# Moving nine wide adjacency checks from VectorE in layer 0 to ScalarE in layers 2 and 3 of a four-layer graph network kernel

## The chip, the cores and the metric

The kernel runs on one core of a Trainium2 chip. The time is the device time of one launch in microseconds (us); several runs of a kernel give a median. A profiled execution has a time of its own and a span, which goes from its first to its last recorded instruction.

The engines are named as in the profile: PE (TensorE; PEld is its weight load), DVE (VectorE), ACT (ScalarE), POOL (GpSimd) and SP (SyncE, which here only issues transfers). Each engine works through its own queue in order: an instruction that waits holds up everything behind it on that engine.

## The reference, cut to what matters

A matrix `x` of 4096 rows and 64 columns goes through four layers of the form x = x + f(relu(layernorm(x)), adj). All four use the same 4096 x 4096 matrix `adj` of zeros and ones.

```python
# layer 0: attention masked by adj, rows scaled by their Lorentz norm
att = sigmoid((2 + 2 * (qm @ k.T)) / att_scale + att_bias)
support = (adj * att) @ h
x = x + support / denorm
# layer 1: entry j of a row weighs 0.5 ** (number of nonzero entries behind it), the last 100 count
x = x + (w @ (h @ weight) + bias)
# layer 2
Ax = adj @ h
x = x + (1.0 - 0.1 * h - 0.01 * sum(h * Ax, axis=1))
# layer 3
nb = adj @ h / maximum(deg, 1)
x = x + relu(concat([h, nb]) @ W.T)
```

## The kernel before

**Two models and a flag.** The kernel holds two versions of the network. The first keeps `adj` on the chip in an 8-bit form and relies on all entries being 0 or 1. The second takes any entries, and runs only if a flag says that some entry is neither. With these inputs it doesn't run. The flag needs each of the 256 tiles of `adj` (128 by 512 entries, f32) to be read once more in full precision and tested. Such a test is called a check. `fetch` (L426) takes the next tile from the deque `checks` and puts its load on SP's queue: one tile of 256 KB into a buffer `ck`, or two at once, 512 KB, into `ckw`. In the last stage the idle space of `s2a` gives two more wide buffers, so some wide checks appear in the profile as `s2a<-s2a`. `check` (L446) keeps loads ahead (three, and four in the last stage) and then has DVE test the oldest one with one instruction, which writes a count into a column of `odd`.

**Layer 0** goes over eight blocks `ib` of 512 rows (7 down to 0), each in 16 steps `g` of two 128-row tiles; the counter `k` numbers these 128 steps. A step has scores on PE (`ps`, L1059), a sigmoid on ACT (into `ps`, or into `att` for the first step in a group of four), a product with the mask on DVE, and, one group later, the sum on PE (`acc`, L1090). Three PSUM tiles hold the scores. `rows0` (L1020) turns the sums of a finished block into new rows, with small work on PE, ACT, DVE and POOL spread over the steps of the next block. POOL also issues the loads of the masks, one in each step (`load_masks`, L208). From step 33 on, the loop calls `check()` at five of every eight steps (L1234), narrow ones: 60 in all.

**Layer 1** counts and weighs entries (`cnt` L1500, `acc` L1535). `rows1` (L1314) makes the rows of a finished block and, in the same go, the inputs `s23` of layers 2 and 3. It is a chain over PE, ACT, POOL and DVE with three products of its own on PE (`pr`, `ph`, `pn`). It runs partly under the next stage.

**Layers 2 and 3** are summed together. `both_layers` (L1629) is one PE product (L1632), 1024 in all. `both_summed` (L1697) takes the row tiles in 16 pairs: the first six side by side over the first 28 of 32 steps, then each to its end, then the others one after another. The pairs use seven PSUM banks in turn. `need(2, t)` (L387) holds the writing of the program at step t until `rows1` of that block has been written out. After every eighth product `beat` (L1615) moves the pending jobs by one step, and at every second beat asks for one wide check on DVE. `last_rows` (L1657) finishes a pair: `high` on ACT, `agg`, `high`, `y` on DVE, `xm` on ACT, `y` on DVE, then the store.

**The flag.** `flagged` (L1287) is put among the jobs when the twelfth pair is written. When no check is left it sums `odd` into `bad` on DVE, four steps later PE adds it over the partitions (`pf`), DVE makes the flag, and all engines load it (L1725) while PE sums the last tile.

The program is written in a fixed order by hand (a manual schedule), so the order of the Python calls is the order on each queue. Almost all DVE and ACT instructions are recorded through one helper and carry its line, L73; they are told apart by their tiles.

Of the kernel before, what the change touches and what calls it, by code (L numbers as in the profile page):

```python
# [11 lines left out]
F32 = mybir.dt.float32  # L12
BF16 = mybir.dt.bfloat16
# [3 lines left out]
AF = mybir.ActivationFunctionType  # L17

GUESS, SHARE = 515594453.0, 0.0624625
ALU = mybir.AluOpType  # L20
AX = mybir.AxisListType
# [4 lines left out]
D = 64  # L26
P = 128
NT = N // P
IB = 512
NIB = N // IB  # L30
CI = IB // P
CG = 2
NG = NT // CG
# [45 lines left out]
def kernel(  # L79
# [12 lines left out]
    nc = tc.nc  # L92

    cpool = ctx.enter_context(tc.tile_pool(name="const", bufs=1))
# [19 lines left out]
    one = cpool.tile([P, 1], F32, name="one")  # L114
    nc.vector.memset(one, 1.0)
    eps = cpool.tile([P, 1], F32, name="eps")
    nc.vector.memset(eps, EPS)
    eps_up = cpool.tile([P, 1], F32, name="eps_up")
    nc.vector.memset(eps_up, EPS / UP / UP)

# [46 lines left out]
    def model(general):  # L167
# [4 lines left out]
        dve = Planned(nc.vector, clock, 0.07, 0.00105)  # L172
        act = Planned(nc.scalar, clock, 0.12, 0.00072)

        def pool(name, bufs, on=stack, **kw):
            return on.enter_context(tc.tile_pool(name=name + sfx, bufs=bufs, **kw))
# [25 lines left out]
        def get_mask(mp, ib):  # L202

            masks[ib] = mp.tile([P, NT, IB], FP8, name=f"mask{ib}{sfx}")
# [35 lines left out]
        def small(name, tag, on=epi, n=CI):  # L240
            return on.tile([P, n], F32, tag=name, name=f"{name}{tag}{sfx}")
# [128 lines left out]
        def push(job, lag):  # L370

            jobs.append([job, lag])
# [20 lines left out]
        def drain():  # L393
            while jobs:
                step()
# [9 lines left out]
        checks = deque(() if general else range(NIB * NT))  # L405
# [18 lines left out]
        fetched, made = deque(), [0]  # L424
# [21 lines left out]
        def check(tiles=1):  # L446


            for _ in range(1 if tiles == 1 else ahead[0] - len(fetched)):
                fetch(tiles)  # L450
            if fetched:
                k, at = fetched.popleft()
                dve.scalar_tensor_tensor(
                    at, at, 0.0, at, ALU.not_equal, ALU.not_equal, accum_out=odd[:, made[0] : made[0] + 1]
                )
                made[0] += 1
# [612 lines left out]
        def sigmoids(ps, to=None):  # L1069

            to = ps if to is None else to
            act.activation(to, ps, AF.Sigmoid, bias=att_c, scale=att_a)
            return to
# [119 lines left out]
        with tc.manual_schedule():  # L1193
            acc, late = first_rows_and_block()
            push(rows0(order0[0], evacuated(order0[0], acc, 0)), 10)
            pro_stack.close()
            mp1 = pool("mask_b", 1, side="right")
            for ib in order0[EARLY:]:
                get_mask(mp1, ib)
            spare.append(pool("pp1", 1, l0, space=PSUM))  # L1200
            if not general:
                push(count_constants(), 1)
            asking = iter(())

            def on():
                step()
                next(asking, None)

            sizes = [2] * 8 if general else [4] * 4
            first = [2] * 7 if general else [4, 4, 3, 3]
            sizes = first + (NIB - 2) * sizes + [0]
            k, done = NG + 2, NG
            LEAVING = {112 - 4 * ib: ib for ib in range(NIB)}
            for size in sizes:
                now = []
                for n, (ib, g) in enumerate(todo[k : k + size]):
                    edge[0] = n == size - 1
                    ps = scores(ib, g)  # L1220

                    if size > 2 and not now:
                        att = frm = sigmoids(ps, att_tile(ib, g))
                    else:
                        frm, att = sigmoids(ps), att_tile(ib, g)
                    masked(ib, g, frm, att)
                    now.append((ib, g, att))
                    load_masks(1)
                    k += 1
                    if k == 92 and not general:  # L1230
                        push(count_constants_2(), 1)
                    if not general and k in LEAVING:
                        taken(LEAVING[k])
                    if k > 2 * NG and k % 8 in (0, 2, 4, 5, 7):  # L1234
                        check()
                    on()
                for ib, g, att in late:
                    at = done % NG
                    if at == 0:
                        acc = pa0.tile([P, IB], F32, tag="pa", name=f"acc0_{ib}{sfx}")  # L1240
                        if ib > 0:
                            asking = queries(ib - 1)
                    gather(acc, fb, g, att, at)
                    if at == NG - 1:
                        push(rows0(ib, evacuated(ib, acc, 0)), 10)
                    done += 1
                late = now
            edge[0] = True
            if len(checks) % 2:
                check()  # L1250
            if general:
                drain()
# [12 lines left out]
        evac = pool("evac", 1)  # L1265
# [21 lines left out]
        def flagged(flag):  # L1287

            steps = 7 if general else 4
            while checks or fetched:  # L1290
                yield
            bad = small("bad", "")[:, 0:1]
            dve.tensor_reduce(bad, odd, AX.X, ALU.add)
            for _ in range(steps):
                yield
            pf = pm.tile([P, CI], F32, tag="pr", name="pf")
            nc.tensor.matmul(pf[0:1, 0:1], bad, one, start=True, stop=True)
            yield
            dve.tensor_scalar(flag, pf[0:1, 0:1], 1.0, None, ALU.min)
# [227 lines left out]
        with tc.manual_schedule():  # L1527
# [45 lines left out]
            late, k, moved, due = None, 0, False, 0.0  # L1573
# [38 lines left out]
        SKEW = 1  # L1612
        summed, beats = [0], [0]

        def beat():  # L1615
            step()
            beats[0] += 1
            if beats[0] % 2:
                check(2)

        flag, any_odd = None, []

        LEAD, SPLIT, PAIR = 6, 28, 2
        BANKS = (2, 5, 6, 0, 1, 3, 4)
# [32 lines left out]
        def last_rows(acc, tiles, tag, begun=None):  # L1657

            n, last = len(tiles), begun is not None
            h, xm = begun or rows_begun(tiles, tag)  # L1660
            high, agg = (
                ends.tile([P, n, 2, D], F32, tag=a, name=f"{a}_{tag}", bufs=2)
                for a in ("high", "agg")
            )
            y = ends.tile([P, n, D], F32, tag=f"y{last}", name=f"y_{tag}", bufs=2)
            inn = ends.tile([P, n], F32, tag="inn", name=f"inn_{tag}", bufs=2)
            act.activation(high, acc[:, 0:n, 0::2, :], AF.Copy, scale=STEP / UP)
            if not last:
                yield
            dve.scalar_tensor_tensor(  # L1670
                agg, acc[:, 0:n, 1::2, :], 1.0 / UP, high, ALU.mult, ALU.add
            )
            if not last:
                yield
            for j, t in enumerate(tiles):
                dve.scalar_tensor_tensor(
                    high[:, j, 0, :], agg[:, j, 0, :], -0.01 / UP, h[:, j, :],
                    ALU.mult, ALU.mult, accum_out=inn[:, j : j + 1],
                )
                dve.scalar_tensor_tensor(  # L1680
                    y[:, j, :], agg[:, j, 1, :], rdegs[:, t : t + 1], fa[:, t, :],
                    ALU.mult, ALU.add,
                )
            if not last:
                yield
            for j in range(n):
                act.activation(xm[:, j, :], xm[:, j, :], AF.Identity, bias=inn[:, j : j + 1])
            if not last:
                yield
            dve.scalar_tensor_tensor(y, y, 0.0, xm, ALU.max, ALU.add)  # L1690
            if not last:
                yield
            rows = slice(tiles[0], tiles[0] + n)
            (nc.scalar if last else nc.gpsimd).dma_start(out=out[:, rows, :], in_=y)
            yield
# [36 lines left out]
        if not general:  # L1732
            with tc.manual_schedule():
                for n in range(2):
                    free = q_sb[:, n * NT // 2 : (n + 1) * NT // 2, :]
                    more.append(free.rearrange("p (c a) d -> p c (a d)", c=CG))
                ahead[0], counting[0] = 4, False
                ends = pool("ends", 1, l2)
                both_summed()
            l2.close()  # L1740
            stack.close()
            return any_odd
# [169 lines left out]
```

## Time and profile before

| what | us |
|---|---|
| median of 3 runs (572.57 to 573.76) | 573.25 |
| the profiled execution | 572.18 |
| its span | 569.5 |
| PE busy | 552.0 (97%) |
| DVE busy | 467.5 (82%) |
| ACT busy | 358.8 (63%) |
| POOL busy | 272.2 (48%) |
| 60 narrow checks on DVE (`ck`) | 42.8, and 4.7 to read their counts |
| 76 wide checks on DVE (`ckw`) | 96.0, and 6.0 |
| 22 wide checks on DVE (`s2a`) | 27.6, and 1.7 |
| 1024 products of layers 2 and 3 (L1632) | 114.0 |

On the time line layer 0 reaches from about 58 to 296 us, layer 1 to about 444, layers 2 and 3 to 563, and the last rows and their stores to the end. PE's share of busy time is modelled and can hide short waits inside a group; waits between groups are shown in brackets on the time line.

### The profile page before, as it was taken

To read this page: it belongs to the slowest core of one execution; us is meant where nothing else is said; L and a number is where in the kernel's file an instruction comes from. 1 tells how busy PE (TensorE), PEld (TensorE's weight loads), DVE (VectorE), ACT (ScalarE), POOL (GpSimd) and SP (SyncE) were. 2 spreads that over 40 slices of the span, in tenths; PEclk is the share of its full clock that TensorE was granted. 3 is DMA by queue.
4 is the path that set the end of the run, shared out by engine and by line. 5 is a ranking of instruction groups with operands and counts; after the bars stand their busy time and mean duration, and the time that the engine had idled before them with its cause. 6 is when DMAs were issued, how large, how long until landed. Compare 5 with 4: busy or idle time off the path is not lost.

```text
span 569.5 us, 9915 instructions
## 1 busy us (share of the span) xinstructions
PE 552.0 (97%) x3368; PEld 280.8 (49%) x3368; DVE 467.5 (82%) x949; ACT 358.8 (63%) x663; POOL 272.2 (48%) x526
## 2 busy tenths in 40 slices
PE   8999999999999999999999999999999999999995
PEld 3563333333333333333334444445454788888884
DVE  4679657799999999898976877778969897799993
ACT  3677667766676776778741888988888432342231
POOL 7624402675757576754444510384634343334332
PEclk9999999999999999999999999999999999999998
DMA  8995952689999999994223465453544788859960
GB/s 145 133 106 47 100 50 20 57 131 154 150 169 150 166 126 173 152 158 121 74 89 113 151 209 168 132 170 112 155 145 132 241 266 304 274 190 323 343 251 21
DMA packets 45612, 87.86 MB, mean 154 GB/s; under 512 B 6272, under 2 KB 24576, under 8 KB 45552
## 3 DMA queue, kind: packets, MB, share of 16 engines
q1 hardware_dynamic: 26112, 69.14, 36.5%
q0 software_dynamic: 18912, 17.77, 33.0%
q8 instruction: 28, 0.46, 0.3%
q10 hardware_dynamic: 528, 0.23, 0.2%
q14 instruction: 32, 0.26, 0.2%
HBM read 135.60 MB, written 1.05 MB: 240 GB/s over the span
## 4 chain that ended last, share of the span: by engine, by line
PE 70%; DVE 13%; POOL 5%; ACT 5%; issue 3%; DMA 2%; DVEq 0%; ACTq 0%; POOLq 0%; SPq 0%
PE acc L1090 15%; PE acc L1632 15%; PE ps L1059 15%; PE acc L1535 8%; PE cnt L1500 8%; PE idle L1183 3%; DVE att L73 3%; DVE ckw L73 2%; PE many L1387 1%; DMA s2a<-adjt_dram 1%; DVE s2a L73 1%; ACT ps L73 1%; DVE rrq L73 1%; POOL mask L211 1%; PE pt L266 1%
## 5 line engine op out<-in xcount | busy, mean ns | idle before, releaser
L1059 PE MATMUL ps<-qt,kt 64*128 64x512 f32 x512 | 123.4, 610 | 3.4 <-DVE att L73 3.0
L1090 PE MATMUL acc<-att,fb 128*64 128x512 f32 x512 | 117.8, 599 | 0.6 <-DVE att L73 0.5
L1632 PE MATMUL acc<-s,mask 128*128 128x256 f16 x1024 | 114.0, 273 | 0.4 <-DVE s L73 0.4
L73 ACT ACTIVATE w<-cnt 128x512 int16<-128x512 f32 x187 | 98.6, 606 | 12.1 <-PE cnt L1500 11.0
L1632 PEld LDWEIGHTS <-mask 128*128 128x128 fp8e4 x1024 | 99.8, 98 | 13.0 <-issue 1.0
L73 DVE TENSOR_TENSOR att<-ps,mask 128x1024 f32<-128x1024 f32 x82 | 98.6, 1217 | 8.6 <-ACT ps L73 8.5
L73 DVE SCALAR_TENSOR_TENSOR ckw<-ckw 128x1024 f32<-128x1024 f32 x76 | 96.0, 1274 | 4.2 <-DMA ckw<-adjt_dram 4.2
L73 ACT ACTIVATE ps<-ps,att_c,att_a 128x1024 f32<-128x1024 f32 x82 | 93.8, 1175 | 1.3 <-PE ps L1059 0.8
L73 ACT ACTIVATE att<-ps,att_c,att_a 128x1024 f32<-128x1024 f32 x46 | 54.6, 1202 | 54.1 <-PE ps L1059 53.9
L1059 PEld LDWEIGHTS ps<-qt,kt 64*128 64x128 f32 x512 | 44.8, 186 | 79.0 <-issue 28.7
L211 POOL DMA_DIRECT2D mask<-adjt_dram x128 | 70.1, 560 | 19.1 <-DMA mask<-adjt_dram 17.4
L73 DVE TENSOR_TENSOR att<-att,mask 128x1024 f32<-128x1024 f32 x46 | 56.9, 1252 | 18.8 <-ACT att L73 18.5
L1500 PE MATMUL cnt<-mask,after 128*128 128x512 fp8e4 x256 | 67.4, 379 | 2.7 <-DVE two L73 0.8
L1090 PEld LDWEIGHTS acc<-att,fb 128*64 128x64 f32 x512 | 33.5, 136 | 73.0 <-issue 67.6
L1535 PE MATMUL acc<-w,s2a 128*128 128x512 bf16 x256 | 66.2, 379 | 1.2 <-ACT asb L73 1.2
L73 DVE TENSOR_SCALAR w<-cnt 128x512 int16<-128x512 f32 x69 | 46.9, 686 | 22.6 <-PE cnt L1500 22.2
L301 POOL TENSOR_TENSOR rs_a<-rs_y 128x4 f32<-128x4 f32 x48 | 19.1, 398 | 67.4 <-DVE rs_y L73 61.0
L73 DVE SCALAR_TENSOR_TENSOR ck<-ck 128x512 f32<-128x512 f32 x60 | 42.8, 713 | 0.0
L1535 PEld LDWEIGHTS <-s2a 128*128 128x128 f16 x256 | 24.6, 98 | 33.6 <-issue 5.6
L1500 PEld LDWEIGHTS <-after 128*128 128x128 bf16 x256 | 24.4, 99 | 31.0 <-issue 2.7
L73 ACT ACTIVATE xm<-xm,inn 128x64 f32<-128x64 f32 x32 | 10.4, 347 | 45.9 <-DVE high L73 44.2
L1183 PE MATMUL idle<-ones 128*128 128x512 bf16 x126 | 30.9, 401 | 1.6 <-DVE ones L73 1.6
(248 smaller groups left out, 611.9 us busy)
## 6 DMA issues: line engine op xcount, KB each, us to landing
ckw<-adjt_dram SPq DMA_DIRECT2D x76, 512.0 KB, 4.3
mask<-adjt_dram POOLq DMA_DIRECT2D x128, 128.0 KB, 8.7
ck<-adjt_dram SPq DMA_DIRECT2D x60, 256.0 KB, 5.9
s2a<-adjt_dram SPq DMA_DIRECT2D x22, 512.0 KB, 4.9
x_sb<-x_dram SPq DMA_DIRECT2D x4, 256.0 KB, 7.5
out_dram<-y POOLq DMA_DIRECT2D x15, 64.0 KB, 3.7
apart_m<-mask SPq DMA_DIRECT2D x16, 16.0 KB, 4.1
mask<-apart_m SPq DMA_DIRECT2D x16, 16.0 KB, 4.3
```

The source lines that it names most:

```text
L73: return op(out, *args, **kw)
L211: nc.gpsimd.dma_start(out=masks[ib][:, g * CG : (g + 1) * CG, :], in_=adjt[ib, g])
L266: nc.tensor.transpose(pt[:, c, :], part, ident)
L301: nc.gpsimd.tensor_tensor(a, y, y, ALU.mult)
L1059: nc.tensor.matmul(ps[:, c, :], kt[half, g, :], qts[ib][half, :], start=True, stop=True)
L1090: nc.tensor.matmul(acc[c * D : (c + 1) * D, :], lhs[:, t, :], rhs[:, c, :], start=(at == 0), stop=(at == NG - 1), skip_group_check=True,)
L1183: nc.tensor.matmul(v.idle[:, v.filling % CG, :], ones, ones.unsqueeze(1).to_broadcast([P, IB // P, P]), start=True, stop=True, skip_group_ ...
L1387: nc.tensor.matmul(pc[q * NT : (q + 1) * NT, :], lane[:, NT - 1 - t : 2 * NT - 1 - t], masks[quad * QUAD + q][:, t, :], start=(t == 0), st ...
L1500: nc.tensor.matmul(cnt, by, what, start=True, stop=True, skip_group_check=True)
L1535: nc.tensor.matmul(accs[ib], apart_s if t < 0 else both(s2a, t), w, start=(t == NT - 1), stop=False, skip_group_check=True,)
L1632: nc.tensor.matmul(acc[:, to, :, :].rearrange("p k d -> p (k d)"), masks[ib][:, t, c * P : (c + 1) * P], s23[:, t, :, :].rearrange("p k d ...
```

## The change

Eighteen of the 60 narrow checks of layer 0 are dropped: the loop checks at seven of every 16 steps, no more ten. The 18 tiles are instead taken from the end of the deque when layers 2 and 3 begin, as nine pairs. For each pair SP loads 512 KB into one buffer `cka`. Five beats later ACT starts four passes over it, each followed by a pause of a beat (the last by none): Relu(a - 1), Relu(-a), Sign(a) and Sign(1 - a), each with a sum over the entries into one column of `act_sums`. The values themselves go to `act_unused`, which shares its space with the buffer `asb` of layer 1. The load of the next pair is written one beat after the last pass, and waits for that pass, as there is one buffer. DVE's checks of layers 1 to 3 stay as they are, 98 wide ones.

The flag takes in the new sums: `flagged` also waits for `tested`, and `oddness` adds six small DVE instructions behind `bad`. To make room, `agg` has one buffer instead of two; it is written and read by DVE alone.

```diff
@@ -115,6 +115,8 @@
+    less = cpool.tile([P, 1], F32, name="less")
+    nc.vector.memset(less, -1.0)
@@ -1231,7 +1233,7 @@
-                    if k > 2 * NG and k % 8 in (0, 2, 4, 5, 7):
+                    if k > 2 * NG and k % NG in (0, 2, 5, 8, 10, 12, 13):
                         check()
@@ -1287,10 +1289,12 @@
-            while checks or fetched:
+            while checks or fetched or not (general or tested):
                 yield
             bad = small("bad", "")[:, 0:1]
             dve.tensor_reduce(bad, odd, AX.X, ALU.add)
+            if not general:
+                oddness(bad)
@@ -1612,13 +1616,54 @@
+        passes = iter(())
+
         def beat():
             step()
             beats[0] += 1
             if beats[0] % 2:
                 check(2)
+            next(passes, None)
 
         flag, any_odd = None, []
+        BY_ACT, FIRST_PASS = 9, 5
+        tested = []
+
+        def tested_by_act():
+            sums = ends.tile([P, 4, BY_ACT], F32, name="act_sums")
+            unused = evac.tile([P, CG * IB], BF16, tag="asb", name="act_unused", bufs=1)
+            for n in range(BY_ACT):
+                k = by_act.pop() - 1
+                by_act.pop()
+                at = ends.tile([P, CG * IB], F32, tag="cka", name=f"cka_{k}", bufs=1)
+                nc.sync.dma_start(out=at, in_=adjt[k // NT, k % NT // CG].rearrange("p c i -> p (c i)"))
+                for _ in range(FIRST_PASS):
+                    yield
+                for m, (func, bias, scale) in enumerate(
+                    ((AF.Relu, less, 1.0), (AF.Relu, 0.0, -1.0), (AF.Sign, 0.0, 1.0), (AF.Sign, one, -1.0))
+                ):
+                    nc.scalar.activation(
+                        unused, at, func, bias=bias, scale=scale, accum_out=sums[:, m, n : n + 1]
+                    )
+                    yield
+                    if m < 3:
+                        yield
+            tested.append(sums)
+
+        def oddness(bad):
+            out, signs = (small(f"act_{a}", "", ends, 1) for a in ("out", "signs"))
+            sums = tested[0]
+            dve.tensor_reduce(out, sums[:, 0:2, :], AX.XY, ALU.add)
+            dve.tensor_reduce(signs, sums[:, 2:4, :], AX.XY, ALU.add)
+            good = float(BY_ACT * CG * IB)
+            dve.tensor_scalar(out, out, 0.0, None, ALU.not_equal)
+            dve.tensor_scalar(signs, signs, good, None, ALU.not_equal)
+            dve.tensor_tensor(bad, bad, out, ALU.add)
+            dve.tensor_tensor(bad, bad, signs, ALU.add)
@@ -1659,8 +1704,8 @@
             high, agg = (
-                ends.tile([P, n, 2, D], F32, tag=a, name=f"{a}_{tag}", bufs=2)
-                for a in ("high", "agg")
+                ends.tile([P, n, 2, D], F32, tag=a, name=f"{a}_{tag}", bufs=bufs)
+                for a, bufs in (("high", 2), ("agg", 1))
             )
@@ -1736,6 +1781,8 @@
                 ends = pool("ends", 1, l2)
+                by_act = [checks.pop() for _ in range(CG * BY_ACT)][::-1]
+                passes = tested_by_act()
                 both_summed()
```

In the built program nothing else moves: PE's and POOL's instructions stand in the same order as before, DVE loses the 18 checks and gains the memset and the six instructions behind `bad`, ACT gains 36 passes between its others and no load of a function table, and SP loses 18 loads of 256 KB in layer 0 and gains nine of 512 KB behind layer 1.

## The prediction

> **What bounds the kernel now.** I read first the busy time by stage (stretch; its length; busy us of PE, PEld, DVE, ACT and POOL; granted clock; DMA share; GB/s).
>
> ```profile
> 183.00:214.00 31.00, 30.38 (x138) 10.56 (x136) 28.29 (x49) 21.08 (x24) 21.28 (x47) 1.00 1.01 153
> ...
> 445.00:480.00 35.00, 34.04 (x314) 29.53 (x312) 30.76 (x67) 10.81 (x58) 12.78 (x15) 1.00 0.85 276
> ...
> 520.00:540.00 20.00, 20.00 (x185) 17.93 (x184) 19.90 (x51) 4.61 (x15) 7.27 (x10) 1.00 0.98 343
> ```
>
> PE sets the pace: one block of layer 0 leaves it 0.6 us idle in 31, the last stage nothing. DVE is nearly full in both. ACT has room in the last stage (4.6 us busy of 20), which is where the passes go; but DMA is full there (0.98), and the passes need loads.
>
> Next, PE's waits in layer 0, on its time line:
>
> ```profile
> 178.62 1.99 PE L1059 MATMUL ps<-qt,kt 64*128 64x512 f32 x8 [0.77 <-DVE att L73]
> ...
> 209.56 1.99 PE L1059 MATMUL ps<-qt,kt 64*128 64x512 f32 x8 [0.62 <-DVE att L73]
> ...
> 264.49 1.99 PE L1059 MATMUL ps<-qt,kt 64*128 64x512 f32 x8 [0.68 <-DVE att L73]
> ```
>
> The name DVE misleads at the first two. The time line of all engines ahead of 209.56:
>
> ```profile
> 204.18 0.67 POOL L332 TENSOR_TENSOR xc<-x_sb,st 128x256 f32<-128x256 f32 x1
> ...
> 204.88 0.42 ACT L73 ACTIVATE sq<-xc 128x256 f32<-128x256 f32 x1 [1.88 <-POOL xc L332]
> ...
> 206.39 1.22 DVE L73 TENSOR_TENSOR att<-ps,mask 128x1024 f32<-128x1024 f32 x1 [0.89 <-ACT ps L73]
> ```
>
> POOL's `xc` is late, behind five mask issues (2.7 us from 201.48); ACT's `sq` waits for it, two sigmoids stand behind `sq`, and DVE itself waits 0.89 us before the product that PE needs. At 264.49 it is DVE: a check stands directly ahead of the product (262.54, 0.74 us).
>
> Third, the seam into layers 2 and 3, where the chain of waits runs through DVE and one load:
>
> ```profile
> 445.64 8.09 DMA s2a<-adjt_dram
> ```
>
> and on the time lines of ACT and PE:
>
> ```profile
> 450.47 0.42 ACT L73 ACTIVATE s<-fa 128x256 f32<-128x256 f32 x1 [4.61 <-POOL fa L332]
> 450.79 0.35 ACT L73 COPY ht<-ph 128x256 f32<-128x256 f32 x1
> ```
>
> ```profile
> 452.21 0.71 PE L1367 MATMUL pn<-wln_sb,ht 64*128 64x128 f32 x8
> ```
>
> PE needs `ht` 1.07 us after ACT has it. Last, the flag, on the time line of the end:
>
> ```profile
> 555.18 0.34 DVE L73 TENSOR_REDUCE bad<-odd 128x1 f32<-128x176 f32 x1
> ...
> 556.05 0.09 PEld L1297 LDWEIGHTS pf<-one,bad 128*1 128x1 f32 x2 [0.21 <-issue]
> ```
>
> `bad` is ready 0.5 us before PE takes it, and 64 products (7.1 us) and the tail (6.2 us) stand behind `pf`. DVE has had no pause since 510.
>
> **Layer 0: gain 1.5 us (0 to 5.5).** Eighteen checks of 0.713 and 0.079 us are 14.2 us of DVE. What PE can gain is far less. From the transposes of one block to the next take 30.36, 31.09, 30.94, 31.32 and 31.02 us, together 154.7; PE's own work in a block is 4 x 7.22 (a group of scores and one of sums) + 0.96 (transposes) = 29.84, five times 149.2. So 5.5 us is the ceiling. Dropped are, of each 16 steps, the checks behind steps 3, 6 and 14 counted from 0. Behind step 6, DVE then only waits longer at step 8 (0.66 us now, for ACT and so for PE). The chain that ends at 209.50 starts from that step, through two kept checks, `rs_y`, and POOL; a shorter DVE before and after moves nothing in it. I count the wait at 264.49, which has a dropped check right ahead (0.7), and some 0.2 us in each of four blocks where a group of scores takes 3.9 us and not 3.65: 1.5. At the ends of the layer nothing: PE is busy without a pause from 276 to 296. Dropping 18 loads from SP's queue there hides behind the same work, since no mask is waited for.
>
> **The passes as such: 45 us of ACT, hidden.** No row has this pass. The nearest, by form (busy us and mean ns):
>
> ```profile
> L73 ACT ACTIVATE ps<-ps,att_c,att_a 128x1024 f32<-128x1024 f32 x82 | 93.8, 1175 | 1.3 <-PE ps L1059 0.8
> ...
> L73 ACT COPY tq<-ps_q 128x1024 f32<-128x1024 f32 x4 | 4.0, 1012 | 1.3 <-PE ps_q L733 1.3
> ...
> L73 ACT ACTIVATION_READ_ACCUMULATOR s<-fa 128x1 f32 x16 | 3.0, 187 | 0.0
> ```
>
> Bounds are 1.01 and 1.18 + 0.19 = 1.37 us; I take 1.25, as reading the sum partly overlaps the next. 36 x 1.25 = 45 us go into about 76 idle us of ACT (111 less 35 busy). Three passes in a pair of 6.26 us take 3.75, rows 1.75: it fits. If it did not, `high` would be late, then `agg` on DVE, then `bad`.
>
> The Trainium skill ("ScalarE: Activation LUTs", What ACT_TABLE_LOAD costs) gives 186 ns + 0.833 a column, 93 more for a pointer operand, and 93 of overlap. By that an estimate is 0.95 to 1.04 us a pass, 36 us in all, and each stall below 0.2 us shorter. Its Rules for kernel authors also send relu to VectorE, which speaks against this move; what it costs in idle ACT time, the trace here says is nothing.
>
> **The first pass at the seam: loss 4.0 us (0.4 to 6.0).** The load of the first pair goes out right behind the `s2a` load above, at about 446.05. The first pass stands in ACT's queue between the two lines shown, so ACT reaches it at 450.9. It can start when the load is in: 451.0 by the median of such loads (4.9 us), 456.5 if it follows the `s2a` load of 453.73 as that one followed the one before (DVE got that at 450.97, 2.76 earlier). I take one load's 0.52 MB at 0.35 MB/us behind 453.73, so 455.2: the neighbour in the same queue is the nearer row. Pass 1.25 and `ht` 0.35 end at 456.8; PE, waiting with `pn` since 452.21, loses 4.6. Queued behind: on PE all products, on ACT `sq`, the copies, and, behind the second pass, `kept`, which DVE wants at 456.99 and gets near 460.5. So DVE's chain slides too (3.5), and PE's later waits in this stretch (0.53 and 0.43) repay only about 0.6: 4.0. PE has no idle time from 485 to 563 to win it back.
>
> **The end: loss 3.2 us (0.7 to 6.0).** Two things meet. DMA: about three of the nine loads fall into 515 to 535. There 338 GB/s are moved, 6.8 MB; with 1.6 more it is 8.3 MB, which at 0.35 to 0.368 MB/us (the best five us of the stage) takes 22.7 to 23.8 us. From 535 to 550 hardly any room is left. So DVE's last check comes 1.9 to 3.7 us late, taken 2.5. The six instructions behind `bad`: two sums of about 0.2, four small ones at 0.17 to 0.19 and their gaps, 1.2 us. Less the 0.5 us of slack: 3.2. The low end is the six alone; the high end adds 1.5 us of DVE waiting for `high` behind a pass. Behind `pf` nothing is hidden.
>
> The skill ("DMA: Bandwidth & Descriptors", Specifications) puts the limit of one core's reads at about 358 GB/s; the stage's best five us show 368, so it is no strict wall here. By it the checks would come about 3 us late.
>
> `less` hides under the first loads of x; the single `agg` is written and read in DVE's order and costs gaps of 0.04 us at most.
>
> Sum: 572.18 - 1.5 + 4.0 + 3.2 = 577.9. The profiled execution is 1.1 below the median, so the median becomes 578.9.
>
> **Rivals.** *The load is early.* If it lands by 451.3 (the median says so, its neighbour against), the seam costs 0.4: 573.25 - 1.5 + 0.4 + 3.2 = 575.4.
> *Layer 0 pays.* If DVE's backlog, and not POOL, carries PE's pauses from block to block, up to all 5.5 us of excess comes back. For: DVE is 28.3 busy of 31, and the first block with checks throughout ran 0.7 us quicker than the next ones, as if a backlog built up. Against: DVE's own waits of 0.66 and 0.89. Full price with both losses at their low ends: 573.25 - 5.5 + 0.4 + 0.7 = 568.9; with 4.0: 570.4. It decides once the gain passes the losses, so only together with a seam that costs little.
> *SP is held up.* The next `cka` load waits on SP for the last pass, with DVE's loads behind it. DVE's loads have some 0.4 us to spare (three checks of 1.57 us against 4.3 to land), so an ACT that runs 0.8 us behind in eight turns adds up to 8 x 0.4 = 3.2 more, and both ends high: 573.25 - 1.5 + 6.0 + 6.0 + 3.2 = 587.0.
>
> **How the numbers follow.** Forecast 0.56, early load 0.14, layer 0 pays 0.19, SP held up 0.11. Within 0.2% (1.1 us, about what can be told from no change) counts the early load with a short end, 0.06; faster 0.18; slower 0.76. For 8 in 10 I cut the far part of the third case and of the last: 570.8 to 585.0. The forecast's own range, with its three terms halfway to their bounds, is 575 to 582.
>
> **What would show it.** Right: one PE wait of 3 to 6 us at `pn` near 452 put down to ACT `ht`, with ACT idle before the first pass on DMA; waits of DVE for `ckw` or `s2a` loads past 515; PE waiting at `pf` for `bad`; blocks of layer 0 still near 31 us. Wrong: blocks near 30 us, or a first pass that starts at once.

## The result, and the profile after

The changed kernel takes 586.89 us (median of 6 runs, 585.09 to 589.92) against 572.88 for the kernel before in the same runs: 1.0245 times, with a 95% interval of 1.0225 to 1.0265. The forecast was 578.9 us with a range of 570.8 to 585.0: the sign and the places were right, the size was not. The profiled execution took 585.09 us, the shortest of the six, with a span of 583.3, which is 13.8 more than the span before.

First the stretches of the changed kernel, in the columns used above (the stretch, its length, busy us of PE, PEld, DVE, ACT and POOL, granted clock, DMA share, GB/s):

```profile
183.00:214.00 31.00, 30.61 (x138) 10.61 (x134) 27.32 (x43) 21.10 (x24) 20.98 (x48) 1.00 0.96 133
445.00:480.00 35.00, 30.43 (x270) 26.48 (x269) 25.80 (x57) 18.67 (x71) 11.47 (x15) 0.95 0.78 261
520.00:540.00 20.00, 20.00 (x186) 17.93 (x185) 17.71 (x47) 13.34 (x31) 4.38 (x9) 1.00 0.97 374
```

Layer 0 is little changed: DVE has 1 us less to do in 31, and PE is 0.4 us idle, not 0.6. From 445 to 480 PE has lost 3.6 us of work (30.43 busy, 34.04 before) and its granted clock is below 1. From 520 to 540 PE loses nothing, but DVE is 2.2 us less busy than before (17.71, 19.90): it waits, at a time when DMA moves 374 GB/s.

The seam into layers 2 and 3, on the time lines of ACT and then PE:

```profile
453.61 1.15 ACT L1647 ACTIVATE act_unused<-cka,less 128x1024 bf16<-128x1024 f32 x1 [4.70 <-DMA cka<-adjt_dram]
454.66 0.19 ACT L1647 ACTIVATION_READ_ACCUMULATOR act_unused<-cka,less 128x1 f32 x1
454.75 0.35 ACT L73 COPY ht<-ph 128x256 f32<-128x256 f32 x1
```

```profile
455.16 0.89 PE L1371 MATMUL pn<-wln_sb,ht 64*128 64x128 f32 x8 [4.57 <-ACT ht L73]
```

ACT stands 4.70 us before its first pass until the load is in, and PE waits 4.57 us for the `ht` behind that pass. The end, on PE's time line:

```profile
554.73 4.42 PE L1677 MATMUL acc<-s,mask 128*128 128x256 f16 x39
567.29 0.19 PE L1301 MATMUL pf<-one,bad 128*1 128x1 f32 x2 [8.14 <-DVE bad L73]
567.41 9.20 PE L1677 MATMUL acc<-s,mask 128*128 128x256 f16 x64
```

PE waits 8.14 us for `bad`, where it had none to wait for before, and the 64 products behind `pf` take 9.20 us instead of 7.16. So the span's 13.8 us are made up of these: layers 2 and 3 begin 1.70 earlier (442.38, 444.08 before), the last `pn` comes 3.04 later (484.10, 481.06), so the seam cost 4.74; then 8.14 at `pf`, 2.04 in the products behind it and 0.5 in the tail. The sum 3.04 + 8.14 + 2.04 + 0.5 is 13.7.

Why `bad` is late is read from DVE's waits between the start of layers 2 and 3 and `bad` (us in total, times, the longest). Before, then after:

```profile
DVE y L73 <- DMA out_dram<-y: 3.4, 4, 2.2
DVE rs L73 <- ACT rs L73: 1.9, 1, 1.9
DVE s L73 <- POOL s L286: 1.6, 1, 1.6
DVE agg L73 <- ACT high L73: 1.6, 1, 1.6
DVE s2a L73 <- DMA s2a<-adjt_dram: 0.9, 1, 0.9
DVE ckw L73 <- DMA ckw<-adjt_dram: 0.8, 1, 0.8
```

```profile
DVE y L73 <- DMA out_dram<-y: 5.7, 4, 2.0
DVE va L73 <- ACT rs L73: 4.3, 1, 4.3
DVE agg L73 <- ACT high L73: 3.8, 3, 2.0
DVE ckw L73 <- DMA ckw<-adjt_dram: 3.4, 4, 1.2
DVE rs L73 <- ACT rs L73: 1.9, 1, 1.9
DVE s2a L73 <- DMA s2a<-adjt_dram: 1.7, 1, 1.7
DVE s L73 <- POOL s L288: 0.7, 1, 0.7
DVE kept L73 <- ACT kept L73: 0.7, 1, 0.7
```

With the short ones, these come to 10.2 us before and 22.3 after. The way from the start of the stage to `bad` became 12.8 us longer (111.1 to 123.9), so nearly all of it is waiting: 5.0 for what stands on ACT behind the first load (`rs`, `kept`), 3.3 for DVE's own loads, 2.3 for stores of `y`, 2.3 for `high`, less 0.9 for `s`. DVE is the engine that has no room in this stage: its work and these waits fill nearly the whole way, so what it waits longer shows in `bad`. The 8.14 us of PE's wait follow from it: 12.8, and 0.7 for the six instructions behind `bad`, less the 4.74 that PE itself had lost at the seam and the 0.5 of slack before, come to 8.3.

And ACT's longest group of waits after the change, in the same stretch:

```profile
ACT act_unused L1647 <- DMA cka<-adjt_dram: 21.3, 7, 4.7
```

### The profile page after: what moved, and what is told of

It is laid out like the page before. It is cut to its first block, busy times and chain, and to the rows that moved or that the text cites. A ratio compares the mean times of both kernels' runs of the same rounds, so it can differ in the third digit from the quotient of the medians.

```text
span 583.3 us, 9920 instructions
## 1 busy us (share of the span) xinstructions
PE 553.7 (95%) x3368; PEld 283.3 (49%) x3368; DVE 457.7 (78%) x920; ACT 397.9 (68%) x735; POOL 265.0 (45%) x526
## 3 DMA queue, kind: packets, MB, share of 16 engines
HBM read 135.60 MB, written 1.05 MB: 234 GB/s over the span
## 4 chain that ended last, share of the span: by engine, by line
PE 58%; DVE 14%; ACT 9%; DMA 9%; POOL 5%; issue 4%; ACTq 0%; SPq 0%; DVEq 0%; POOLq 0%
PE acc L1092 15%; PE ps L1061 14%; PE acc L1539 8%; PE cnt L1504 8%; PE acc L1677 6%; DMA cka<-adjt_dram 5%; DVE att L73 4%; ACT act_unused L1647 3%; DVE ckw L73 3%; DMA out_dram<-y 2%; PE many L1391 1%; ACT ps L73 1%; DMA vec<-vecs_dram 1%; ACT w L73 1%; PE pr L1326 1%
## 5 line engine op out<-in xcount | busy, mean ns | idle before, releaser
L1677 PE MATMUL acc<-s,mask 128*128 128x256 f16 x1024 | 116.7, 277 | 0.0
L1677 PEld LDWEIGHTS <-mask 128*128 128x128 fp8e4 x1024 | 101.2, 99 | 13.8 <-issue 0.7
L73 DVE TENSOR_TENSOR att<-ps,mask 128x1024 f32<-128x1024 f32 x82 | 98.0, 1218 | 10.2 <-ACT ps L73 9.9
L303 POOL TENSOR_TENSOR rs_a<-rs_y 128x4 f32<-128x4 f32 x48 | 16.7, 347 | 67.5 <-DVE rs_y L73 61.0
L73 DVE SCALAR_TENSOR_TENSOR ck<-ck 128x512 f32<-128x512 f32 x42 | 30.8, 734 | 0.0
L73 DVE SCALAR_TENSOR_TENSOR s2a<-s2a 128x1024 f32<-128x1024 f32 x22 | 27.1, 1242 | 1.7 <-DMA s2a<-adjt_dram 1.7
```

Source lines behind the costliest of these rows:

```text
L73: return op(out, *args, **kw)
L303: nc.gpsimd.tensor_tensor(a, y, y, ALU.mult)
L1677: nc.tensor.matmul(acc[:, to, :, :].rearrange("p k d -> p (k d)"), masks[ib][:, t, c * P : (c + 1) * P], s23[:, t, :, :].rearrange("p k d ...
```

## The experiments

Three explanations of the late `bad` were open. *Loop*: with one buffer, each load is written only after the last pass, ACT then stands before it at the head of its queue (21.3 us in all), and what it owes DVE is late. *DMA*: the nine loads take room that DVE's loads and the stores need. *ACT's time*: the passes themselves are too long. Medians are set against the kernel before in the same set of runs. The last two columns are of the profiled execution alone: for kernels 2, 3, 4 and 10 that was the longest of its runs (1.9, 3.6, 1.8 and 2.5 us above the median), for the change and kernel 8 the shortest (1.8 and 1.3 below). Where kernels of different sets are compared, two differences are given: that of the medians, and that of the column "less before", as the kernel before itself came out between 572.88 and 573.76.

| kernel | median us | less before | ratio, 95% interval | PE waits at pf | 64 products behind |
|---|---|---|---|---|---|
| the change | 586.89 | +14.0 | 1.0225 to 1.0265 | 8.14 | 9.20 |
| 1 layer 0 alone | 572.18 | -1.0 | 0.9966 to 1.0010 | 0.68 | 7.16 |
| 2 loads alone | 578.79 | +5.6 | 1.0056 to 1.0105 | 5.47 | 9.90 |
| 3 passes alone | 572.84 | -0.3 | 0.9967 to 0.9996 | 3.12 | 8.83 |
| 4 two buffers | 588.30 | +15.1 | 1.0219 to 1.0274 | 10.78 | 9.82 |
| 5 four y | 583.68 | +9.9 | 1.0145 to 1.0203 | 5.76 | 9.06 |
| 6 first pass later | 584.18 | +10.4 | 1.0158 to 1.0219 | 9.87 | 8.53 |
| 7 seam, y and flag | 578.99 | +5.2 | 1.0075 to 1.0133 | 3.21 | 10.02 |
| 8 before, four y | 572.87 | -0.9 | 0.9978 to 1.0000 | 0 | 7.16 |
| 9 as 7, passes packed | 580.72 | +7.2 | 1.0110 to 1.0153 | 3.13 | 10.00 |
| 10 the change, wait filled | 584.67 | +11.2 | 1.0170 to 1.0204 | 2.69 | 7.16 |
| 11 six pairs | 573.45 | 0.0 | 0.9986 to 1.0011 | 0 | 7.16 |
| 12 as 7, wait filled | 576.76 | +3.9 | 1.0047 to 1.0088 | 1.52 | 7.16 |

**Kernels 1 to 3: the parts by themselves.** Layer 0 alone:

```diff
-            while checks or fetched or not (general or tested):
+            while checks or fetched:
...
-            if not general:
-                oddness(bad)
...
-                passes = tested_by_act()
```

> The changed kernel with the 18 checks dropped from layer 0 and nothing put in their place: no loads, no passes and no six instructions behind bad, so 18 tiles are not tested at all. All theories of the loss (loop, DMA, ACT's time) expect what the changed kernel's trace shows for layer 0, where layers 2 and 3 began at 442.38 us, not 444.08: 1.7 us less than the kernel before, about 571.2. Had DVE's backlog in layer 0 been the bound (the rival of the prediction), up to 5.5 less, 567.5. It is the base against which the next three are read.

It came to 1.0 us less, with an interval from 1.9 less to 0.6 more. The five and a half us of the rival are excluded, and the 1.7 of the one trace is at the upper side: over the eleven kernels with these 18 checks dropped, layers 2 and 3 begin between 442.4 and 443.9, in the two with the old layer 0 at 444.08 and 443.82, and in kernel 11, with 12 dropped, as late as 445.26. A trace's start of this stage is good to about a us only. The loads alone, with seven beats in place of the passes and, as in kernel 1, without the six instructions:

```diff
-                for m, (func, bias, scale) in enumerate(
...
+                for _ in range(7):
+                    yield
```

> The nine loads of 512 KB at their places in the program, with no passes over them and no six instructions, so 18 tiles are loaded but not tested. Theory loop (the loss at the end comes from one buffer: each load is written only after the last pass, ACT then waits for it at the head of its queue, and high, agg, y and the checks run late): the loads alone cost little, 571.2 plus 0 to 1, and PE waits at pf for less than 1 us. Theory DMA (the loads push DVE's checks back by taking DMA's time): as the prediction priced it, 2.5 less 0.5 of slack, 573.2; if it is the whole loss at the end, 580. Theory ACT's time: 571.2.

6.6 us more than layer 0 alone: not the 2 of the prediction, and near the 580 of a loss that is DMA's alone. ACT does nothing new here, and yet DVE's longest groups of waits are

```profile
DVE y L73 <- DMA out_dram<-y: 6.6, 3, 3.2
DVE ckw L73 <- DMA ckw<-adjt_dram: 2.5, 4, 1.1
```

The larger part is not DVE's loads but its `y`: it has two buffers, so it waits for the store of the pair two ahead. That these stores land later because of the loads is not shown; kernel 3 will show the same waits with one load of the nine. The runs of this kernel spread: the three shortest (575.28 to 576.24) have a mean granted clock of 0.994 to 0.997, the five longest (579.25 to 580.67) 0.989 to 0.992. So a part of the 6.6 goes with PE's clock, to which kernels 10 and 12 come back. The passes alone:

```diff
-            if not general:
-                oddness(bad)
...
+                if n == 0:
...
+                    for _ in range(FIRST_PASS + 7):
+                        yield
+                    continue
```

> One load, long landed when it is first read, and 32 passes over it at the places of the second to the ninth pair; the first pair's four passes and eight of the loads are left out, so of the 18 tiles two are tested eight times and sixteen not at all. The six instructions stay. Theory loop: no wait for a load, so the passes hide; 571.2 plus 0.5 to 1 for the six instructions and up to 1.5 for rows that stand behind a pass: 572 to 574, PE's wait at pf under 2.5 us. Theory ACT's time (32 passes of about 1.27 us are themselves too much for ACT's rows): 578 to 582, with the wait at pf still above 5 us. Theory DMA: 572.

572.84: ACT's time is not the cause. The expectation says that the six instructions stay, but this kernel leaves out their call, and its trace has one `bad` instruction alone; so their price is not in these 0.7 us above kernel 1. The profiled execution, 3.6 us above the median, waits 3.12 at `pf`; such a median leaves no room for that wait in most runs. DVE's longest group of waits in it is

```profile
DVE y L73 <- DMA out_dram<-y: 6.5, 3, 3.1
```

as much as in kernel 2, where kernel 1's trace has 3.7. Long waits for stores come up in single executions without the loads too, so one trace can't put them down to DMA.

**Kernel 4: is it the one buffer?**

```diff
+                if n % 2:
+                    at = more[-1].rearrange("p c i -> p (c i)")
...
+                following = begun(n + 1) if n + 1 < BY_ACT else None
```

> The changed kernel with a second buffer for the pairs (one of the two halves of s2a, so that DVE's wide checks turn over four buffers and not five); each pair's load is written before the four passes over the pair ahead of it, some eleven beats before it is read. All passes, loads and the six instructions are there. Theory loop: ACT no longer waits for loads after the first one, the wait at pf falls from 8.1 us to about 1 and what follows it is not slowed; the seam of 4.7 us stays: 571.2 + 4.7 + 1 to 2 = 577 to 578. Theory DMA: the same bytes move in the same stage, so the end stays late, 584 to 587. Theory ACT's time: 584 to 587 too.

ACT's waits for `cka` fall from 21.3 us to 3.9 and DVE waits no more for `high` ahead of `bad`, but the time is 588.3: taking ACT's waits away doesn't help by itself, against *loop*. DVE's first group of waits has become its own loads:

```profile
DVE ckw L73 <- DMA ckw<-adjt_dram: 10.1, 9, 1.9
```

This kernel takes one of five buffers from DVE's checks, which may be part of these 10.1, so it doesn't exclude *loop* on its own; kernel 9 has all five, but another fault.

**Kernels 5 to 8: the waits of DVE one by one.** Four buffers for `y` (in the changed kernel, and in the one before as kernel 8):

```diff
-            y = ends.tile([P, n, D], F32, tag=f"y{last}", name=f"y_{tag}", bufs=2)
+            on, of, bufs = (ends, f"y{last}", 2)
+            if not last and tag % 4 > 1:
+                on, of, bufs = temps, ("ht", "two")[tag % 2], 1
+            y = on.tile([P, n, D], F32, tag=of, name=f"y_{tag}", bufs=bufs)
```

> The changed kernel with four buffers for y instead of two (the two more take turns with ht and two, which are free by then). Theory DVE is full: from the start of layers 2 and 3 to bad DVE waits 10.2 us in the kernel before and 22.3 in the changed one, and bad is late by the difference; 5.7 of the 22.3 are waits of y for the store of the pair two ahead. Without them bad comes up to 5.7 earlier: PE's wait at pf falls from 8.1 to between 2.4 and 4, and the time from 586.9 to between 580 and 583. Rival, DMA alone: the room that DVE gains there turns into waits for its own loads, 585 to 588. Rival, loop (ACT's late high is what DVE waits for in the end): 584 to 587.

3.2 us less by the medians, 4.1 by the column: near what a full DVE predicts (580 to 583), but above it, as PE's wait of 5.76 is above the 2.4 to 4. The 5.7 us of waits for stores are gone; DVE's wait for `high` grew from 3.8 to 5.4 in their place, and 3.2 us in two waits of `y` have no cause that the profile names.

> The kernel before with four buffers for y. DVE's 3.4 us of waits for stores go, but bad was in time by 0.5 us there and PE had no wait: no change, 573.2 plus or minus 0.6, and bad earlier by up to 3.4 us. Rival: DVE's lateness limits the kernel before as well, up to 3 less, 570.

No change in time that can be told from the kernel before, while `bad` comes 3.8 us earlier:

```profile
551.42 0.34 DVE L73 TENSOR_REDUCE bad<-odd 128x1 f32<-128x176 f32 x1
...
555.42 0.19 PE L1297 MATMUL pf<-one,bad 128*1 128x1 f32 x2
```

The same waits for stores stood in the kernel before and cost nothing, because `bad` was in time. The later first pass:

```diff
-                for _ in range(FIRST_PASS):
+                for _ in range(FIRST_PASS if n else 11):
```

> The changed kernel with the first pass 11 beats behind its load and not 5. Theory seam as the prediction has it: ACT no longer stands before a load at about 450, PE's wait of 4.6 us at pn is gone or under 1, and, as DVE loses its 5.0 us behind the same load too (waits for rs and kept), PE's wait at pf stays near 8: 586.9 less 4.0 to 4.7 gives 582 to 583. Rival: DVE's loss at the seam is not its only one there, the loads behind it take the place, and pf then waits longer: 585 to 587. Rival: the wait at pf is in good part the seam's own loss carried on by DVE, and falls with it to about 5: 579 to 580.

The wait at `pn` near 450 is gone (one of 1.39 us is left, at 475), and the time falls by 2.7 by the medians or 3.6 by the column, not by 4.0 to 4.7, for PE now waits 9.87 us at `pf`: PE regained more at the seam than DVE did, and meets it again at the end. The three edits together (the third moves the sums of the passes ahead of `bad`):

```diff
+            out, signs = (odd[:, made[0] + i : made[0] + i + 1] for i in range(2))
+            made[0] += 2
...
-            dve.tensor_tensor(bad, bad, out, ALU.add)
-            dve.tensor_tensor(bad, bad, signs, ALU.add)
```

> The changed kernel with three edits: first pass 11 beats behind its load, four buffers for y, and the sums of the passes tested ahead of bad and written to two columns of odd, which leaves one instruction and not seven in front of pf. Theory DVE is full: 586.9 less 4.4 for the seam, less 4 to 5.7 for the stores, less 0.8 for the six instructions, less about 2 since PE's clock no longer falls behind a long wait: 574 to 577, the rest being DVE's loads (3.3) and high (2.3). Theory DMA alone: 580 to 583.

579.0, between the two theories. The wait at `pf` is down to 3.21, but the products behind it still take 10.02.

**Kernels 9 and 11: loop or DMA for the rest.** Packed passes, with later first passes:

```diff
-        BY_ACT, FIRST_PASS = 9, 5
+        BY_ACT, FIRST_PASS = 9, 8
...
-                    if m < 3:
-                        yield
```

> The kernel of the run before last (first pass 11 beats behind its load, four buffers for y, the sums tested ahead of bad), with each later pair's first pass 8 beats behind its load and not 5, and its passes in beats that follow each other. There ACT waited 12.6 us for loads and DVE 6.9 us for high behind it, and PE 3.2 us at pf. Theory loop, for this rest: with 3 beats more, most loads are in when ACT comes to them, DVE's wait for high falls towards the 1.6 of the kernel before, bad comes 3 to 5 us earlier and is in time: 579.0 less 3.2 and less the 2.9 us that the 64 products behind pf took above 7.16: 572.5 to 575. Rival ACT's time: four passes in a row (5 us) hold high up as the wait did: 577 to 580.

A miss: no faster than kernel 7 (1.7 us slower by the medians, with intervals that overlap). ACT's waits for `cka` did fall, from 12.6 to 2.4, and DVE's for `high` from 6.9 to 4.3, so the rival, four passes in a row that hold `high` up, isn't it either. But DVE's waits for its own loads rose from 4.3 to 9.4, here with all five buffers:

```profile
DVE s2a L73 <- DMA s2a<-adjt_dram: 4.8, 6, 2.4
DVE ckw L73 <- DMA ckw<-adjt_dram: 4.6, 5, 1.7
DVE agg L73 <- ACT high L73: 4.3, 4, 1.9
```

The packed passes also hold up an `ht` at 477 (PE waits 2.72 at `pn`). Why DVE's loads are late here is to be seen on SP. It stands before the load of `cka` until ACT's pass is over, with DVE's loads behind it in the queue; of SP's waits, in the changed kernel and then in this one:

```profile
SPq L1641 <- ACT act_unused L1647: 12.4, 6, 3.5
```

```profile
SPq L1639 <- ACT act_unused L1645: 27.8, 6, 5.9
```

In kernel 7 it is 9.2. Of the 9.4 us that DVE waits for its loads, 6.2 are for loads issued within 1.4 us behind a load of `cka` for which SP had stood 3.0 to 5.8 us. That is what the prediction's rival of an SP that is held up describes. In the changed kernel 3.4 of DVE's 5.1 us are of this kind (behind waits of SP for ACT of 0.3 to 4.0 us). In kernels 2 and 4 SP waits for no pass, and DVE waits for loads all the same: in kernel 2 these land 6.5 to 7.3 us after their issue, against a median of 5.2 for `ckw` before. So the traces show both, loads that are issued late and loads that land late, and no run parts them. That ACT's loads push DVE's back by DMA's room alone is not shown by kernels 4 and 9. Six pairs, 10 beats ahead:

```diff
-                    if k > 2 * NG and k % NG in (0, 2, 5, 8, 10, 12, 13):
+                    if k > 2 * NG and k % NG in (0, 2, 5, 8, 10, 12, 13, 15):
...
-        BY_ACT, FIRST_PASS = 9, 5
+        BY_ACT, FIRST_PASS = 6, 10
```

> As the kernel with packed passes, but six pairs and not nine (12 of the 60 checks dropped from layer 0, not 18), a pair's first pass 10 beats behind its load and a beat of pause after each pass again. Three loads of 512 KB less and none that ACT has to wait for: PE's wait at pf is under 1 us and the seam costs nothing; the gain in layer 0 is two thirds of the 1.0 to 1.7 us: 572.3 to 573.2, level with the kernel before or 0.2% below. Rival: DMA, the six loads still push DVE's checks back by more than the 4 us that y's buffers gain: 575 to 578.

`bad` is in time: 573.45, level with the kernel before. Against kernel 7 two things differ, three loads fewer and the longer lead of each; which of them did it isn't shown. DVE still waits 7.1 us for loads, but none for stores or `high`, 11.0 in all. So two thirds of the work can be moved at no cost, and nothing was gained by it: what layer 0 gives is about the noise.

**Kernels 10 and 12: the products behind the wait.** PE is given 72 products that nobody reads (28 in kernel 12) ahead of `pf`:

```diff
+                for _ in range(72):
+                    nc.tensor.matmul(
+                        fill.rearrange("p k d -> p (k d)"), masks[0][:, 0, 0:P],
...
```

> The changed kernel with 72 products more on PE directly ahead of pf, into a bank that nobody reads, which fill the time in which it waited for bad (8.1 us at 0.112). Nothing else is changed and bad comes when it came. Theory clock: the 64 products behind pf took 9.20 us and not 7.16 because PE had stood still; with PE busy they take 7.2 again and the time falls by 2 to 2.6, 584.3 to 585. Rival: they are slow for another reason (what DMA, DVE and ACT do at that time), 9.2 stays, 586.5 to 588.

2.2 us less than the change by the medians, 2.8 by the column, though nothing is done earlier; and the mean granted clock of its runs is 0.989 to 0.995, that of the change's 0.981 to 0.987. The stretches of the changed kernel, then of this one; the clock is the third number from the right:

```profile
565.00:570.00 5.00, 2.71 (x15) 1.94 (x16) 3.62 (x19) 1.58 (x6) 1.96 (x5) 0.50 0.05 15
570.00:575.00 5.00, 5.00 (x40) 4.19 (x39) 1.24 (x6) 1.58 (x5) 1.10 (x3) 0.84 0.06 18
```

```profile
565.00:570.00 5.00, 2.90 (x27) 2.34 (x24) 4.93 (x16) 1.89 (x6) 1.14 (x1) 1.00 0.02 6
570.00:575.00 5.00, 4.40 (x42) 3.93 (x43) 2.53 (x16) 1.29 (x4) 2.50 (x8) 1.00 0.06 18
```

In the changed kernel PE comes back from its wait to half the clock; here the clock stays at 1.00, and the 64 products take 7.16.

> The kernel with the later first pass, four buffers for y and the sums tested ahead of bad (579.0 us), and 28 products more on PE ahead of pf, which fill the 3.2 us in which it waited there. Theory clock: the products behind pf, 10.02 us in that run, take 7.2 again, and the time falls by up to 2.9 though nothing is done sooner: 576 to 577. Rival: the wait is too short to matter for the clock, or the filling only delays pf where bad is early: 578.5 to 580.

The 64 products take 7.16 here too, not 10.02. In time it is 2.2 us less than kernel 7 by the medians and 1.3 by the column, with intervals that just overlap.

## Why the prediction was wrong

- **Layer 0, gain 1.5:** right in kind and nearly in size. Layers 2 and 3 begin 1.70 earlier in the trace, the time by itself is 1.0 less, and PE's five blocks take 152.6 us together, not 154.7: 30.5 each, between the signs for right (31) and wrong (30).
- **The passes as such, 45 us, hidden:** right. A pass takes 1.054 us (1.148 with a pointer as bias) and 0.187 for its sum, 1.25 to 1.3 each, and 32 of them without new loads cost 0.7 us, within the noise.
- **The first pass at the seam, loss 4.0:** right, slightly small. The wait at `pn` is 4.57 against 4.6 foretold, net 4.74: the eight products behind it took 1.89 us and not 1.05, at a clock of 0.59 from 455 to 458. The step did see that DVE's chain slides too, but took this for settled at the seam. It is not: DVE has no room to win it back, and of the seam's 4.7 us only 2.7 to 3.6 came off when it was removed (kernel 6).
- **The end, loss 3.2 (0.7 to 6.0): this is the step that failed,** by its size. It measured 8.14 + 2.04 + 0.5 = 10.7, against 3.2. It named DMA as the cause, and kernel 2 shows the loads alone making `bad` late. But it counted only DVE's own checks: 2.5 (its own division gives 2.7 to 3.8, not 1.9 to 3.7), measured 3.3, of which 2.2 past 515. The stores of `y`, 2.3 us more and in kernel 5 worth 3.2 to 4.1, weren't in it, though the trace before had the 3.4 us of waits for them; why they grew is open. `high`, 2.3, stood only in its high end with 1.5. The six instructions were 0.7, foretold 1.2. And the slower products, 2.0 and more, were in no term. And DMA was less busy after the change, not fuller, where the step had it run out of room, from 515 to 535 (before, then after):

```profile
515.00:535.00 20.00, 20.00 (x186) 17.93 (x185) 19.86 (x57) 4.80 (x16) 6.78 (x9) 1.00 0.95 338
```

```profile
515.00:535.00 20.00, 20.00 (x186) 17.92 (x184) 17.60 (x48) 11.88 (x27) 5.26 (x9) 1.00 0.84 312
```

It moved less there, not 1.6 MB more. DVE was late by then (its seventh store of `y` is issued at 519.03, not 511.85), and the bytes came behind: from 555 to 560 DMA moves 392 GB/s, where it moved 15 before.

- **The rival "SP is held up"** gave 587.0, next to the 586.9 that came. Its mechanism is there: SP waits 12.4 us for passes, and 3.4 of DVE's 5.1 us of waits for loads stand behind such a wait. But DVE's waits for loads grew by 3.3 us in all, and the rest of the loss, stores, `high`, the seam and the clock, has other names; with two buffers SP waits for no pass and the time is no better, with loads alone there is none to wait for and 6.6 us are lost. So the nearness of the number is in part luck, and its share is open.
- **The other signs foretold** came: the wait at `pn`, ACT idle before its first pass, DVE waiting for loads past 515, PE waiting for `bad`. They told the places, not the sum.

What stays open: how the end's loss divides between DMA's room, ACT's standing before loads and SP's standing before passes. The kernels that take one away (4 and 9) bring in another cost, so no sum of single parts gives it: alone, layer 0, loads and passes come to -1.0 + 6.6 + 0.7 = 6.3 us, together 14.0. The six instructions, 0.7 in the trace, are in none of the three; the other 7 appear only where the passes and fresh loads are together.

## What to carry to other kernels

When an engine without room sets the end of a stage, sum up all that it waits for there, stores and other engines' results among it: a transfer that is added can reach it by several of these ways, and waits that cost nothing before were already there to be read. A wait that disappears from one queue can turn up in another, as in kernels 4 and 9: look also at the queue that issues the loads, where a load that waits until its buffer has been read holds up all loads behind it. And price PE's waits by the clock behind them, not by their length alone.

## What had not been expected of the hardware

PE's granted clock after a wait. Behind waits at `pf` of 0, 0.68, 1.52 and 2.69 us the 64 products took 7.16 us each time; behind 3.12 to 10.78 us they took 8.53 to 10.02, whatever the length. So the step of the cost lies near 3 us, and is about 1.4 to 2.9 us high; it isn't sharp, for the wait of 2.72 us in kernel 9 was followed by a clock of 0.50 from 477 to 480. The Trainium skill ("TensorE: Matmul & The Clock Gate", What's actually happening) has this: an idle window of about 3.4 us halves the clock until a busy one has passed. The rows agree with the half and with the length, save that waits of 2.72 and 3.12 us already did it.

DMA moved 374 GB/s over 20 us and 417 over 5 (534 to 539), more than the 368 that the prediction had for the stage's best five. That 368 was not the best of the kernel before either: there it moved 381 from 480.5 to 485.5.
